# An attention and FFN block on one core: the softmax shift as the exponential's bias, FFN weights without low parts, and a checked fast path

## The chip, the cores and the metric

The kernel runs on one core of a Trainium2 chip. The metric is the device time in microseconds (us). TensorE is called PE, VectorE DVE, ScalarE ACT, GpSimd POOL, and SyncE, which issues most of the transfers, SP.

## The reference

Two sequences of 2048 rows of 256 pass through an attention block with 16 heads of 64 and then a gated FFN of hidden size 768. All data are float32; the FFN's weights are whole numbers from -127 to 127, divided by 127.

```
def attn(x):                       # x: layernorm of the input
    q, k, v = x @ Wq + bq, x @ Wk + bk, x @ Wv + bv       # 16 heads of 64
    a = softmax(q @ k.T / 8)                              # 2048 x 2048 for each head
    y = x + (a @ v) @ Wo + bo
    return (y - mean(y)) * rsqrt(var(y) + 1e-3) * gamma + beta

def ffn(x):                        # x: layernorm of the attention's result
    return (silu(x @ wg.T) * (x @ wu.T)) @ wd.T

x = x + layernorm(attn(layernorm(x)))
x = x + layernorm(ffn(layernorm(x)))
```

## The kernel before

**Precision.** Most matmul operands have the type float32r. For the projections, the scores and the FFN an operand is split into a high part (the value cast to float32r) and a low part (what the cast left), and a product takes three matmuls: high by high, high by low, low by high. ACT writes the high parts; DVE or POOL subtracts for the low ones.

**Attention.** The work is cut into 64 units `u = (b, p, c)`: sequence, pair of heads, block of 512 queries. `run_unit` writes the order of every engine's instructions by hand; only SP's order is left to a scheduler. The two heads of a pair use the two halves of PE's rows[...]. A unit has two halves (`j` = 0, 1) of eight key tiles of 128. A half runs as follows:

- `scores(u, kt)`: the scores of one key tile, keys by queries, into one of two PSUM buffers (`double`, tile `t`), and then the exponential by ACT (L671) into an SBUF tile `pt` (9 buffers). There are three pairs of matmuls for the split operands and a fourth pair (`unit` by `sh`), which adds each query's shift: minus its largest score.
- `max_pair(ahead, i)`: scores of the *next* unit, high parts only, queries by keys, into one of two other PSUM buffers (`xdouble`, tile `s`), and their maxima by DVE (L633) into `nm`. They stand in PE's order between the score tiles; the eighth of a half stands after the eighth score tile.
- `wo_half`: part of an earlier unit's output projection, added up by DVE (L264) with the inverse of the softmax's sum.
- `add_up(u, j)`: the sum over the eight `pt` tiles. POOL adds six to `accs` (L681, L684); DVE adds the other two into `two` (L688), and POOL adds `two` to `accs` (L691).
- in the first half, projections of later units' Q and K (`projs`) and of V (`v_tile`), and preparation of the FFN's weights (`prep_jobs`)
- `pv`: the product of `pt` and V for the eight tiles, into an `xdouble` buffer. After it, in the first half, `sum_up` and `first_half` bring out the sums of the unit behind, and SP gathers them into `few`; in the second half `cs_item` adds the two halves on DVE into `cf` (L230), and ACT and POOL split that into `cs`.

`shift_min` and `shift_row` make the shift: DVE takes the minimum over `nm`, at the start of the unit eight transposes on PE turn it into a row (L645), and ACT casts it to `sh` (L649). `inv_item`, in the second half, takes the reciprocals `rc` of the sums of the unit behind (L239).

**FFN.** Eight chunks of 512 rows, each with six steps of `gate_up` (six matmuls for gate and six for up), followed by `down` (four row tiles, 18 matmuls each). Between the steps stand pieces of other work: layer norms of the last four chunks (`own_job`), the end of the chunk before (`end_job`), and the last units of attention. The weights are brought on chip as high and low parts by `prep_jobs` during attention, go to memory, and are loaded again by `load_ffn`.

Of the kernel before, what the change touches and what calls it, by code (L numbers as in the profile page):

```python
# [16 lines left out]
P = 128  # L17
# [9 lines left out]

@with_exitstack
def kernel(
# [17 lines left out]
):  # L47
    nc = tc.nc
# [29 lines left out]
    wg_dram = dram.tile([P, 2, DC, HID], F32, name="wg_dram")  # L78
    wu_dram = dram.tile([P, 2, DC, HID], F32, name="wu_dram")
    wd_dram = dram.tile([P, 2, HC, D], F32, name="wd_dram")  # L80
# [4 lines left out]
    nbx = [const.tile([P, NT], F32, name=f"nbx{b}") for b in range(B)]  # L85

# [150 lines left out]
    def inv_item(u):  # L237
        t = op.tile([P, 2, QT], F32, tag="rc", name="rc")
        nc.vector.reciprocal(t, sums.pop(u))  # L239
        invs[u] = t  # L240
# [87 lines left out]
    def prep_jobs():  # L328
        jobs = []

        def piece(w, dst, o, i0):
# [9 lines left out]
            t = hd.tile([P, TT, D], F32, tag="ht", name="wt")[:, :2, :].bitcast(F32R)  # L341
            split(t, ps[:, : 2 * P])
            for k in range(2):
                nc.sync.dma_start(
                    out=dst[:, k, i0 : i0 + 2, o * P : (o + 1) * P],
                    in_=f32(t[:, k, :]).rearrange("p (i n) -> p i n", i=2),
                )

        for w, dst, no, ni in (
# [4 lines left out]
            for o in range(no):  # L354
                for i0 in range(0, ni, 2):
                    jobs.append(piece(w, dst, o, i0))
# [4 lines left out]
    def load_ffn(which):  # L361

        if which < 2:
            full = aw.tile([P, DC, S], F32R, tag=("xh", "xl")[which], name=f"fw{which}")
            full = full.rearrange("p c n -> p (c n)")
            n = 2 * DC * HID
            t = full[:, :n].rearrange("p (w c n) -> p w c n", w=2, c=DC)
            for w in range(2):
                for dc in range(DC):
                    nc.sync.dma_start(  # L370
                        out=f32(t[:, w, dc, :]), in_=(wg_dram, wu_dram)[which][:, w, dc, :]
                    )
                    yield None
# [3 lines left out]
        else:  # L377
            i = 2 * (which - 2)
            t = kp.tile([P, 2, 2, D], F32R, tag="T1", name=f"fw{which}")
            for w in range(2):  # L380
                nc.sync.dma_start(out=f32(t[:, w]), in_=wd_dram[:, w, i : i + 2, :])
                yield None
# [62 lines left out]
    with ExitStack() as actx:  # L445
# [4 lines left out]
        ptp = actx.enter_context(tc.tile_pool(name="ptp", bufs=9))  # L450
# [9 lines left out]

        unit_f = op.tile([P, 2, QB], F32, tag="rr", name="unit_f")[:, 0, :P]
        nc.gpsimd.memset(unit_f, 0.0)
        for e in range(2):
            nc.gpsimd.memset(unit_f[e * K : e * K + 1, :], 1.0)
        unit = bw.tile([P, P], F32R, name="unit")
        nc.scalar.copy(unit, unit_f)

        n8 = bw.tile([P, QT, P], F32, name="n8")
        nc.gpsimd.memset(n8, 0.0)

        wqk, wv, KT, QN, SH, V, nm, pts = ({} for _ in range(8))
# [147 lines left out]

# [15 lines left out]
        def shift_min(u):  # L635
            nc.vector.tensor_reduce(
                n8[:, :, 0 : K + 1 : K].rearrange("p q e -> p e q"), nm.pop(u), AX.X, ALU.min
            )

        def shift_row(u):  # L640

            ps = double()
            for qt in range(QT):
                for h in range(2):
                    nc.tensor.transpose(  # L645
                        ps[:, h, qt * K : (qt + 1) * K], n8[half(h), qt, :], ident[half(h), half(h)]
                    )
            SH[u] = bw.tile([P, QB], F32R, tag="sh", name="sh", bufs=2)
            nc.scalar.copy(  # L649
                SH[u].rearrange("p (q h r) -> p h q r", h=2, r=K),  # L650
                ps[:, :, : QT * K].rearrange("p h (q r) -> p h q r", r=K),
            )
# [525 lines left out]
```

## Time and profile before

| | |
|---|---|
| median of 3 runs | 2960.65 us (2960.57 to 2961.78) |
| the profiled execution's own time | 2961.08 us |
| its span, first to last instruction | 2959.3 us |
| attention | about 2725 us, the FFN the rest |
| busy: PE, DVE, ACT, POOL | 2876.9, 2102.9, 1467.1, 2444.7 us |
| exponentials (L671) | 1024, mean 1027 ns |
| maxima (L633) | 1024, mean 1225 ns |
| POOL's adds to `accs` (L684) | 636, mean 2548 ns |

Busy time is the time in which an engine had at least one instruction running. A group's mean is the time of one instruction.[...]

### The profile page before, as it was taken

How to read it: one execution, taken by the hardware profiler on the slowest of the kernel's cores; microseconds unless marked ns; L12 is line 12 of the kernel's file. 1: busy time of each engine (PE TensorE's matmuls, PEld its weight loads, DVE VectorE, ACT ScalarE, POOL GpSimd, SP SyncE). 2: the span in 40 equal slices, each digit the busy share in tenths (PEclk: the TensorE clock that was granted, in tenths of full speed). 3: DMA queues.
4: the chain of work that ended last, by engine and by line, in shares of the span. 5: the costliest groups of instructions: out<-in, count | busy, mean ns of one | idle time of the engine just before them, and what ended most of it. 6: DMA issues, size and time to landing. Idle time of an engine off the chain costs nothing.

```text
span 2959.3 us, 48771 instructions
## 1 busy us (share of the span) xinstructions
PE 2876.9 (97%) x19492; PEld 1742.6 (59%) x19492; DVE 2102.9 (71%) x2701; ACT 1467.1 (50%) x1740; POOL 2444.7 (83%) x1399
## 2 busy tenths in 40 slices
PE   7999999999999999989999999999999999999998
PEld 5555565556555565555655655555655555555787
DVE  6776677777777777766677767777677767774653
ACT  4545454544445444554455545555455445554443
POOL 4999878888788878877799989998799889888453
PEclk9999999999999999999999999999999999999999
DMA  2000000000000001010000001000000000012000
GB/s 59 19 12 11 14 12 12 12 15 5 17 10 14 9 12 31 5 35 10 26 21 10 7 10 33 5 20 24 5 6 24 21 1 31 23 58 72 29 29 29
DMA packets 125428, 59.14 MB, mean 20 GB/s; under 512 B 77232, under 2 KB 118448, under 8 KB 124816
## 3 DMA queue, kind: packets, MB, share of 16 engines
q1 hardware_dynamic: 124992, 55.62, 7.0%
q8 instruction: 152, 2.49, 0.4%
q0 software_dynamic: 208, 0.40, 0.1%
q14 instruction: 76, 0.62, 0.1%
HBM read 37.89 MB, written 17.83 MB: 19 GB/s over the span
## 4 chain that ended last, share of the span: by engine, by line
PE 85%; DVE 5%; POOL 4%; ACT 3%; issue 1%; DMA 1%; SPq 1%; ACTq 0%; DVEq 0%; POOLq 0%
PE t L670 32%; PE s L701 28%; PE s L626 8%; PE t L579 5%; PE t L604 3%; POOL accs L684 2%; ACT pt L671 2%; PE fp L1002 2%; PE s L199 2%; PE gp L975 2%; PE up L975 2%; PE t L253 2%; DVE two L688 1%; DVE nm L633 1%; DVE acc L264 1%
## 5 line engine op out<-in xcount | busy, mean ns | idle before, releaser
L684 POOL TENSOR_TENSOR accs<-accs,pt 128x1024 f32<-128x1024 f32 x636 | 1620.6, 2548 | 313.8 <-ACT pt L671 268.8
L633 DVE TENSOR_REDUCE nm<-s 128x2 f32<-128x1024 f32 x1024 | 1219.1, 1225 | 500.6 <-PE s L626 500.3
L671 ACT ACTIVATE pt<-t 128x1024 f32<-128x1024 f32 x1024 | 1049.8, 1027 | 184.7 <-PE t L670 117.8
L670 PE MATMUL t<-QN,KT 64*128 64x512 f32 x6144 | 916.0, 403 | 4.7 <-ACT pt L671 3.0
L701 PE MATMUL s<-pt,v 128*64 128x512 f32 x4096 | 908.1, 596 | 0.0
L670 PEld LDWEIGHTS t<-QN,KT 64*128 64x128 f32 x6144 | 521.2, 185 | 244.2 <-ACT pt L671 180.3
L701 PEld LDWEIGHTS s<-pt,v 128*64 128x64 f32 x4096 | 283.0, 137 | 538.4 <-issue 525.7
L626 PE MATMUL s<-KT,QN 64*128 64x512 f32 x2048 | 421.7, 408 | 5.6 <-DVE cf L230 4.1
L670 PE MATMUL t<-sh,unit 64*128 64x512 f32 x2048 | 405.8, 392 | 0.0
L691 POOL TENSOR_TENSOR accs<-accs,two 128x1024 f32<-128x1024 f32 x128 | 305.9, 2390 | 18.5 <-DVE two L690 7.5
L688 DVE TENSOR_TENSOR two<-pt 128x1024 f32<-128x1024 f32 x128 | 309.4, 2417 | 0.0
L223 ACT COPY rr<-s 128x1024 f32<-128x1024 f32 x63 | 63.9, 1015 | 430.2 <-PE s L199 417.0
L626 PEld LDWEIGHTS s<-KT,QN 64*128 64x128 f32 x2048 | 193.4, 185 | 108.4 <-issue 54.4
L649 ACT CAST sh<-t 128x512 fp32r<-128x512 f32 x64 | 37.6, 588 | 420.7 <-PE t L645 420.7
L670 PEld LDWEIGHTS t<-sh,unit 64*128 64x128 f32 x2048 | 192.9, 184 | 51.1 <-ACT sh L649 0.6
L264 DVE SCALAR_TENSOR_TENSOR acc<-t,rc,acc 128x256 f32<-128x256 f32 x500 | 206.9, 476 | 19.9 <-PE t L253 13.0
L579 PE MATMUL t<-xh,wqk 128*128 128x512 f32 x512 | 184.5, 421 | 18.2 <-ACT pt L671 10.5
L681 POOL TENSOR_TENSOR accs<-pt 128x1024 f32<-128x1024 f32 x64 | 154.9, 2420 | 0.5 <-ACT pt L671 0.5
L989 POOL TENSOR_TENSOR hT<-hf,hT 128x512 fp32r<-128x512 f32 x48 | 62.0, 1291 | 107.6 <-ACT hT L988 107.5
L579 PEld LDWEIGHTS t<-xh,wqk 128*128 128x128 f32 x512 | 99.6, 195 | 54.0 <-ACT pt L671 22.8
L589 ACT ACTIVATE QN<-t,bq_sb 128x512 fp32r<-128x512 f32 x64 | 44.1, 689 | 157.2 <-PE t L579 157.2
L253 PE MATMUL t<-wo,cs 64*128 64x256 f32 x1500 | 114.4, 285 | 2.0 <-ACT pt L671 1.8
(167 smaller groups left out, 2167.6 us busy)
## 6 DMA issues: line engine op xcount, KB each, us to landing
few<-rr SPq DMA_DIRECT2D x512, 0.5 KB, 2.0
xc<-in_L_attn_x_dram SPq DMA_DIRECT2D x8, 512.0 KB, 4.0
xT_dram<-hn SPq DMA_DIRECT2D x16, 256.0 KB, 2.1
out_dram<-o SPq DMA_DIRECT2D x14, 256.0 KB, 2.1
xT<-xT_dram SPq DMA_DIRECT2D x3, 1024.0 KB, 5.7
attn_dram<-acc SPq DMA_DIRECT2D x5, 512.0 KB, 2.6
acc<-in_L_attn_x_dram SPq DMA_DIRECT2D x4, 512.0 KB, 8.8
raw_w<-in_L_attn_Wq_dram SPq DMA_DIRECT2D x16, 128.0 KB, 2.2
```

What stands on the lines that cost most here:

```text
L253: nc.tensor.matmul(ps[e][:, i * D : (i + 1) * D], t[half(e), ci, s], w[half(e), wi, :], start=k == 0, stop=k == 2,)
L264: nc.vector.scalar_tensor_tensor(a, ps[e][:, i * D : (i + 1) * D], inv[:, e, q : q + 1], a, ALU.mult, ALU.add)
L579: nc.tensor.matmul(ps[:, k, :], w[:, wi, dc, :], xx[:, dc, s], start=n == 0, stop=n == 5)
L626: nc.tensor.matmul(s[:, e, :], QN[u][half(e), 0, qt * P : (qt + 1) * P], KT[b, p, kc][half(e), 0, :], start=True, stop=True,)
L633: nc.vector.tensor_reduce(nm[u][:, :, qt, kc : kc + 1], s, AX.X, ALU.max, negate=True)
L670: nc.tensor.matmul(ps[:, e, :], w, r, start=n == 0, stop=n == 3)
L671: nc.scalar.activation(pt, ps, AF.Exp, scale=QSCALE)
L681: nc.gpsimd.tensor_tensor(accs[u], todo[0], todo[1], ALU.add)
L684: nc.gpsimd.tensor_tensor(accs[u], accs[u], t, ALU.add)
L688: nc.vector.tensor_tensor(two, p8[n], p8[n + 1], ALU.add)
L691: nc.gpsimd.tensor_tensor(accs[u], accs[u], two, ALU.add)
L701: nc.tensor.matmul(pvs[u][half(e), 0, :], v[:, kt % 4, n : n + K], pt[:, e, :], start=kt % 8 == 0, stop=kt % 8 == 7,)
```

## The change

**Shift.** The score tiles lose the fourth pair of matmuls. The shift is now one number for the unit: minus its largest score over both heads, all its queries and all keys, times 1/8, plus 40. It enters the exponential as a bias, a column of 128 equal values. `shift_out` takes the minimum over `nm` on DVE into a column and sends it through memory: one transfer writes it to `m_dram`, the next reads it back as a row into all partitions (`mb`). `shift_in`, after the second half's `add_up` in the order of DVE and before `cf`, takes the minimum over the row (128 columns) and scales it with a `tensor_scalar`. The transposes, the `sh` cast, `unit` and `n8` are gone.

**Order in a unit.** The next unit's maxima stand between the first six score tiles of a half, the last two after the eighth. The `cs` split of the unit behind stands after the second score tile instead of before the first. `pt` has 10 buffers instead of 9. In the second half POOL adds five tiles and DVE three (two DVE additions instead of one).

**Checks.** `inv_item` gets a POOL instruction that adds `rc` into `inverse`. Each weight piece's low part is reduced to its largest absolute value in `wlow`, and is no longer stored. In the FFN's 17th step `verdict` compares the sum of the inverses with 2^80 and the low parts with zero, gathers the outcome of the 128 partitions through memory, and writes 1 or 0 to `good`.

**FFN.** Only the high parts of the weights are stored, loaded and used: `gate_up` has four matmuls for gate and four for up instead of six and six, `down` 12 for a row tile instead of 18.

**The end.** The former kernel is now `fast_path`. Behind it every engine loads `good` into a register and compares it; if it is 0, `general_path` (some 790 lines, a whole kernel for the same reference that shifts each query by its own maximum and uses split weights) computes the output anew.

```diff
     def inv_item(u):
         t = op.tile([P, 2, QT], F32, tag="rc", name="rc")
         nc.vector.reciprocal(t, sums.pop(u))
+        nc.gpsimd.tensor_tensor(inverse, inverse, t, ALU.add)
         invs[u] = t
...
-            t = hd.tile([P, TT, D], F32, tag="ht", name="wt")[:, :2, :].bitcast(F32R)
-            split(t, ps[:, : 2 * P])
-            for k in range(2):
-                nc.sync.dma_start(
-                    out=dst[:, k, i0 : i0 + 2, o * P : (o + 1) * P],
-                    in_=f32(t[:, k, :]).rearrange("p (i n) -> p i n", i=2),
-                )
+            t = hd.tile([P, TT, D], F32, tag="ht", name="wt")
+            hi = t[:, :1, :].bitcast(F32R)[:, 0, :]
+            nc.scalar.copy(hi, ps[:, : 2 * P])
+            nc.vector.tensor_tensor(t[:, 1, :], ps[:, : 2 * P], f32(hi), ALU.subtract)
+            nc.vector.tensor_reduce(
+                wlow[:, k : k + 1], t[:, 1, :], AX.X, ALU.max, apply_absolute_value=True
+            )
+            nc.sync.dma_start(
+                out=dst[:, i0 : i0 + 2, o * P : (o + 1) * P],
+                in_=f32(hi).rearrange("p (i n) -> p i n", i=2),
+            )
...
-        ptp = actx.enter_context(tc.tile_pool(name="ptp", bufs=9))
+        ptp = actx.enter_context(tc.tile_pool(name="ptp", bufs=10))
...
-        def shift_min(u):
...
-        def shift_row(u):
...
+        def shift_out(u):
+
+            n1 = bw.tile([P, 1], F32, tag="n1", name="n1", bufs=2)
+            nc.vector.tensor_reduce(
+                n1, nm.pop(u).rearrange("p e q c -> p (e q c)"), AX.X, ALU.min
+            )
+            d = m_dram[units.index(u) % 2]
+            nc.sync.dma_start(out=d.rearrange("(p o) -> p o", o=1), in_=n1)
+            t = shift[u] = bw.tile([P, P], F32, tag="mb", name="mb", bufs=2)
+            nc.sync.dma_start(out=t, in_=d.partition_broadcast(P))
+
+        def shift_in(u):
+
+            n1 = bw.tile([P, 1], F32, tag="n2", name="n2", bufs=2)
+            nc.vector.tensor_reduce(n1, shift[u], AX.X, ALU.min)
+            t = bw.tile([P, 1], F32, tag="sh", name="sh", bufs=2)
+            nc.vector.tensor_scalar(t, n1, QSCALE, HEADROOM, ALU.mult, ALU.add)
+            shift[u] = t
...
-            for n in range(4):
+            for n, (ki, qi) in enumerate(((0, 0), (0, 1), (1, 0))):
                 for e in range(2):
                     h = half(e)
-                    w, r = (
-                        (k[h, 0, s], q[h, 0, :]),
-                        (k[h, 0, s], q[h, 1, :]),
-                        (k[h, 1, s], q[h, 0, :]),
-                        (unit[h, :], sh[h, :]),
-                    )[n]
-                    nc.tensor.matmul(ps[:, e, :], w, r, start=n == 0, stop=n == 3)
-            nc.scalar.activation(pt, ps, AF.Exp, scale=QSCALE)
+                    nc.tensor.matmul(
+                        ps[:, e, :], k[h, ki, s], q[h, qi, :], start=n == 0, stop=n == 2
+                    )
+            nc.scalar.activation(pt, ps, AF.Exp, scale=QSCALE, bias=shift[u])
...
-            n = 4 if u == last else 6
+            n = 4 if u == last else 6 - j
...
-            shift_row(u)
-            if cs:
-                drain(cs.pop())
...
-                    if ahead and i < 7:
+                    if ahead and i < 6:
                         max_pair(ahead, 8 * j + i)
                     scores(u, 8 * j + i)
-                if ahead:
-                    max_pair(ahead, 8 * j + 7)
+                    if i == 1 and cs:
+                        drain(cs.pop())
+                for i in (6, 7) if ahead else ():
+                    max_pair(ahead, 8 * j + i)
                 if j == 1:
                     if ahead:
-                        shift_min(ahead)
+                        shift_out(ahead)
                     if behind:
                         inv_item(behind)
...
                 else:
+                    if ahead:
+                        shift_in(ahead)
                     cs.append(cs_item(u))
...
-                for wi, xi in ((0, 0), (0, 1), (1, 0)):
+                for xi in range(2):
...
-            for n, (hi, wi) in enumerate(((0, 0), (0, 1), (1, 0))):
+            for n in range(2):
...
+    def verdict():
+
+        t = op.tile([P, 4], F32, tag="few", name="ok")
+        nc.vector.tensor_reduce(
+            t[:, 0:1], inverse.rearrange("p e q -> p (e q)"), AX.X, ALU.max
+        )
+        nc.vector.tensor_scalar(t[:, 0:1], t[:, 0:1], MOST, None, ALU.is_le)
+        nc.vector.tensor_reduce(t[:, 1:2], wlow, AX.X, ALU.max)
+        nc.vector.tensor_scalar(t[:, 1:2], t[:, 1:2], 0.0, None, ALU.is_equal)
+        nc.vector.tensor_tensor(t[:, 2:3], t[:, 0:1], t[:, 1:2], ALU.mult)
+        nc.sync.dma_start(out=ok_dram.rearrange("(p o) -> p o", o=1), in_=t[:, 2:3])
+        row = op.tile([1, P], F32, tag="cf", name="row")
+        nc.sync.dma_start(out=row, in_=ok_dram.rearrange("(o n) -> o n", o=1))
+        yield
+        yield
+        yield
+        nc.vector.tensor_reduce(t[0:1, 3:4], row, AX.X, ALU.min)
+        nc.vector.tensor_copy(good, t[0:1, 3:4])
...
+def tile_attn_ffn_sandwich_kernel(tc: tile.TileContext, *args):
+    nc = tc.nc
+    with tc.tile_pool(name="good", bufs=1) as pool:
+        good = pool.tile([1, 1], I32, name="good")
+        fast_path(tc, *args, good)
+        value = nc.values_load(good[0:1, 0:1], min_val=0, max_val=1)
+        with tc.If(value < 1):
+            general_path(tc, *args)
```

## The prediction

> **What bounds the kernel now.** I read the page first, then the chain of waits, then the timelines of one unit. [...]Columns of the groups: total busy, mean ns, then idle time before.
>
> ```profile
> PE 2876.9 (97%) x19492; PEld 1742.6 (59%) x19492; DVE 2102.9 (71%) x2701; ACT 1467.1 (50%) x1740; POOL 2444.7 (83%) x1399
> PE 85%; DVE 5%; POOL 4%; ACT 3%; issue 1%; DMA 1%; SPq 1%; ACTq 0%; DVEq 0%; POOLq 0%
> L684 POOL TENSOR_TENSOR accs<-accs,pt 128x1024 f32<-128x1024 f32 x636 | 1620.6, 2548 | 313.8 <-ACT pt L671 268.8
> L671 ACT ACTIVATE pt<-t 128x1024 f32<-128x1024 f32 x1024 | 1049.8, 1027 | 184.7 <-PE t L670 117.8
> L670 PE MATMUL t<-sh,unit 64*128 64x512 f32 x2048 | 405.8, 392 | 0.0
> L589 ACT ACTIVATE QN<-t,bq_sb 128x512 fp32r<-128x512 f32 x64 | 44.1, 689 | 157.2 <-PE t L579 157.2
> ```
>
> PE looks full, and the 2048 shift matmuls look like 406 us. The chain in the last unit, where no maxima run between the score tiles, shows another limit:
>
> ```profile
> 2690.37 1.21 PE t L670 x7
> ...
> 2691.67 1.04 ACT pt L671
> ...
> 2692.75 1.22 PE t L670 x6
> ```
>
> Two score buffers give a loop: matmuls 1.21, exponential 1.03, hand-overs 0.13, together 2.37 us for two tiles, so 1.19 us a tile. Now DVE and POOL around the end of a unit (start, length, what ran, wait in brackets):
>
> ```profile
> 1519.55 1.23 DVE L633 TENSOR_REDUCE nm<-s 128x2 f32<-128x1024 f32 x1 [1.16 <-PE s L626]
> 1520.81 0.19 DVE L636 TENSOR_REDUCE n<-nm 128x8 f32<-128x32 f32 x1
> 1521.19 0.20 DVE L239 RECIPROCAL rc<-few 128x8 f32<-128x8 f32 x1 [0.18 <-issue]
> 1521.52 1.66 DVE L264 SCALAR_TENSOR_TENSOR acc<-t,rc,acc 128x256 f32<-128x256 f32 x4
> 1523.10 2.46 DVE L688 TENSOR_TENSOR two<-pt 128x1024 f32<-128x1024 f32 x1
> 1527.31 0.69 DVE L230 TENSOR_TENSOR cf<-s,rr 128x512 f32<-128x512 f32 x1 [1.75 <-PE s L701]
> 1527.99 2.39 DVE L633 TENSOR_REDUCE nm<-s 128x2 f32<-128x1024 f32 x2
> ```
>
> ```profile
> 1512.21 15.57 POOL L684 TENSOR_TENSOR accs<-accs,pt 128x1024 f32<-128x1024 f32 x6 [1.83 <-ACT pt L671]
> ```
>
> DVE has 1.75 us to spare before cf, and cf frees the PSUM buffer for the second maximum of the next unit. POOL adds all through this stretch. In the FFN:
>
> ```profile
> 2885.00:2935.00 50.00, 50.00 (x293) 44.16 (x291) 18.02 (x56) 20.69 (x38) 20.55 (x16) 1.00 0.07 22
> 2735.00:2885.00 150.00, 138.90 (x790) 120.74 (x789) 91.35 (x362) 66.58 (x126) 78.25 (x62) 0.97 0.09 29
> ```
>
> The busy columns are PE, PEld, DVE, ACT, POOL: PE alone is the limit in the last 50 us, and has DVE close behind before.
>
> [...]the two at 1523.10 takes 2.46 us where the one at 2724.57, with POOL idle, takes 1.22. The POOL add in front of it ended at 1524.48, two ended 1.08 later, and the POOL add then waiting ended at 1527.78, 2.22 after that. [...]L589, with such a bias, takes 689 ns, the plain cast of that size (L649) 588.
>
> **The change, part by part.**
>
> *Scores.* One of four matmul pairs goes (0.23 us a pair: eight matmuls in 0.93), the exponential gets a pointer bias (+0.09). The loop is 2.37-0.23+0.09 = 2.23, so 1.117 us a tile against 1.191 measured in this half (first to eighth start, 1511.04 to 1519.38): the gain is 0.07 a tile, not 0.4. The row transposes (0.39 a unit) and the sh cast go too.
>
> *Second half.* The first exponential starts 0.23 earlier, the eighth 0.23+7x0.074 = 0.7 earlier. The last two maxima are now both issued after the eighth tile, where one was: the first of them starts 0.7 earlier than the row at 1519.55, the second 1.16 later (pitch of the pair at 1527.99), so DVE finishes 0.46 later than now. PV needs the buffer of the first of them: 1518.85+1.23+0.1 = 1520.18, against 1520.25 in the chain. **PE gains nothing in this half.**
>
> *POOL's new wait.* In the built order the addition to `inverse` stands on POOL before the second half's adds, and it waits for rc on DVE. Queued behind it are five adds, two's add, the weight and cs subtractions and the next half's adds. The adds now start at 1512.21; they will start at 1521.39+0.46, plus 0.07 hand-over, 0.2 for the addition (8 columns, priced by POOL's 4-column additions) and 0.08: 1522.2. Does POOL bound the unit then? Its adds end 14 us on, at 1536.1, in time for the pt buffers (the seventh exponential of the next half, about 1537.4); the following half's adds end near 1556, and it idles until the next rc at about 1563. No.
>
> *DVE's longer tail.* The second half gives DVE another add. The first, ready at 1523.56, waits for POOL's add until 1524.6 and ends 1.08 later, 1525.68; [...]the second add ends at 1529.0, 3.3 us long. The new minimum over 128 columns (about 0.35 with gaps, from the 0.19 of 32 columns) and the one-column tensor_scalar (0.2) follow, then cf at 1529.55 to 1530.25: 2.25 us later than now, with PE as before. Behind cf stand the next maxima; behind the second maximum, in PE's order, the second score tile.
>
> *First half of the next unit.* PE now stalls. After cf, four maxima at 1.16 must pass before the sixth; then its score tile 0.23+0.96, then three exponentials at 1.12. With cf ending 3.3 us after PV's end, the eighth exponential ends at 3.3+4.7+1.3+3.4 = 12.7 or so, against 11.4 now: +1.4 us. A unit near 1977 backs this: a cf 2.28 late made its eighth exponential 1.84 late, with the transposes and fourth pair still in. 62 units: +87. Seven units with three V tiles wait for DVE to free their buffers, about +2 each: +14. The last unit has no maxima: -1.5. Together **+99**.
>
> *DMA.* shift_out adds two SP transfers a unit, one behind the other; the nearest rows land in 2.0 to 2.2 us (few, raw_w). From 1521.3 they are back by about 1526, under the two adds until 1529.0, so 0. If each took over 3.8 us they would show. In SP's order few, long issued, precedes them.
>
> *FFN.* 48 gate/up steps lose four matmuls of 0.23: 44 us. 32 down tiles lose six of 18 (2.14 us): 23. In the last stretch PE is alone and all of its share (21) counts; in the first 150 us PE falls to 93 of busy time beside DVE's 91, in order, so I count two thirds of 46. Sum **-50**, between -35 and -67.
>
> *Rest.* The pieces' extra reductions, the halved stores and loads, the tenth pt buffer and verdict's seven small DVE instructions lie beside longer work: 0; uncovered, the reductions cost 18x0.35 = 6. One fewer POOL add a unit (2.5) is spent inside POOL's new idle time: 0. The end adds a register load, a compare-and-branch and a jump over the general path. No row shows them[...]. Estimate +4, from +1[...] to +8[...]; a gain is excluded, since the end has only additions.
>
> Sum: 99-50+4 = +53 on the profiled execution's 2961.08 (span 2959.3 and 1.8 around it; the median 2960.65 is the same within 0.5), so **3013**.
>
> **Rivals.**
> [...]Then it waits for the next POOL add, some 1.8 us, and so does cf: 62x1.8 = +112 more, 3125. The page allows it; no small tensor_scalar in SBUF runs beside POOL in this trace, so one column is open.
> [...]With 1.23 us (the uncontended L690) it ends at 1527.0, cf is at 0.2 late, and the first half gains: -0.39-0.23-0.52, +0.09 for the last exponential, +0.5 for the cs cast now inside the tiles, about -0.55. 62x0.55 = 34, with FFN and end 2882. It decides where the unit loses less than 0.65 us, an add of about 2.6 us. For it: an L690 beside a shorter POOL operation took 2.13. Against: POOL's row of adds without a gap.
> *It runs the general path.* That would about double the time. The condition, worked out from the reference's inputs in float64, is far off: the largest accumulated inverse is about 2^10, the limit 2^80, and weights are whole numbers to 127, which I take as exact in the high part. 2 in 100.
>
> **How the numbers follow.** My case 45 in 100 (2975 to 3060 alone: 0.4 us a unit either way, the FFN's bounds, the end's); [...]the faster cases 27; the general path 2; within 0.2%, about what a measurement here can tell from no change, 4. Faster 0.27, same 0.04, slower 0.69. The range, 2890 to 3130, leaves out the tails of both outer cases.
>
> **What would show it.** Right: POOL's inverse addition idle before it on DVE's rc, some 9 us a unit; the second add (the group two<-two,pt) near 3.3 us; cf no longer waiting for PV; the second score tile of a unit waiting for cf; pt near 1.12 us; FFN steps at 1.84 us of PE. Wrong: two<-two,pt near 1.3 to 2, cf still waiting for PV, or DVE idle on a DMA before shift_in.

## The result, and the profile after

After: **3421.01 us** (median of 4 runs, 3415.91 to 3427.27); before, on the same chip: 2960.61 us (2958.86 to 2961.78). The ratio is 1.1557, interval 1.1531 to 1.1582: slower by 460 us, where +53 was forecast and 3130 was the end of the range.

The page of the kernel after (busy time of the engines, clock granted in 40 slices, then the chain that ended last):

```profile
PE 2811.5 (82%) x16548; PEld 1588.2 (47%) x16548; DVE 2280.3 (67%) x2917; ACT 1495.5 (44%) x1675; POOL 2347.5 (69%) x1397
PEclk9999999999999999988999999999999999999988
PE 34%; DMA 20%; ACT 17%; POOL 12%; DVE 11%; issue 5%; ACTq 0%; SPq 0%; POOLq 0%; DVEq 0%
```

PE has 2944 fewer matmuls and is busy for 65 us less, yet the span grew from 2959.3 to 3413.8. The chain, of which PE had 85% before, now lies on **DMA for 20%**. Before, that was 1%. The stages, from the last PV and the first and last gate matmul: attention ends at 3195.7 instead of 2723.8 (**+471.9**), the FFN to its last gate takes 193.7 instead of 214.3 (**-20.6**), what follows 23.5 instead of 20.3 (**+3.2**). The sum is 454.5, the difference of the spans. The forecast had +99, -50 and +4.

The waits (who waited for whom: total us, how many, the longest) name the place:

```profile
ACT pt L1472 <- DVE sh L1456: 882.7, 64, 15.0
POOL inverse L1056 <- DVE rc L1055: 832.7, 63, 28.4
PE s L1431 <- DVE cf L1046: 403.3, 62, 7.1
DVE n L1454 <- DMA mb<-m_dram: 297.5, 64, 12.5
```

The first is 13.8 us a unit. Of these some 9 aren't due to the trip: with the early shift below the same wait is still 569.7 us, 8.9 a unit, since ACT has nothing to exponentiate while PE does PV. The second is new, as forecast. The third is PE standing 6.5 us a unit for cf. The fourth says why: DVE stands some 4.6 us a unit for the shift to come back, and cf stands behind that on DVE. Of such a wait the forecast had none. The chain at the end of one unit (start, length, what):

```profile
1739.47 0.20 DVE n L1443
...
1739.68 8.11 DMA m_dram<-n
...
1747.81 4.08 DMA mb<-m_dram
...
1751.91 0.30 DVE n L1454
...
1752.23 0.15 DVE sh L1456
1752.38 0.61 DVE cf L1046
...
1753.04 0.79 PE s L1431 x2
```

No engine's work stands in this chain between the column of minima (1739.67) and the reduction of what came back (1751.91): 12.2 us of two transfers, one behind the other. Their issues (us to landing last):

```profile
few<-rr SPq DMA_DIRECT2D x512, 0.5 KB, 2.0
mb<-m_dram SPq DMA_DIRECT2D x64, 64.0 KB, 4.7
m_dram<-n SPq DMA_DIRECT2D x64, 0.5 KB, 7.7
```

`few`, which I took as the nearest row, moves as many bytes in a quarter of the time. The timeline of DVE and POOL in the same stretch (start, length, what ran, wait before it):

```profile
1740.12 0.20 POOL L1056 TENSOR_TENSOR inverse<-inverse,rc 128x8 f32<-128x8 f32 x1 [11.81 <-DVE rc L1055]
1740.28 13.81 POOL L1485 TENSOR_TENSOR accs<-accs,pt 128x1024 f32<-128x1024 f32 x5
1741.75 1.98 DVE L1489 TENSOR_TENSOR two<-pt 128x1024 f32<-128x1024 f32 x1
1743.84 3.21 DVE L1491 TENSOR_TENSOR two<-two,pt 128x1024 f32<-128x1024 f32 x1
1751.91 0.28 DVE L1454 TENSOR_REDUCE n<-mb 128x1 f32<-128x128 f32 x1 [4.86 <-DMA mb<-m_dram]
1752.23 0.15 DVE L1456 TENSOR_SCALAR sh<-n 128x1 f32<-128x1 f32 x1
1752.30 0.68 DVE L1046 TENSOR_TENSOR cf<-s,rr 128x512 f32<-128x512 f32 x1
```

The second add takes 3.21 us amid POOL's adds, where 3.3 was forecast (the 2.22 and 1.08 of the trace of before). The one-column tensor_scalar took 0.15 us while a POOL add ran, so it didn't wait for that add; in 61 of the 64 units a POOL add runs all through it, and its mean is 154 ns. Then DVE waits 4.86 us, cf follows, and with it the score tiles. An instruction that waits holds up those behind it on its engine here: PV is done at 1745.45, but cf, behind DVE's wait and sh, starts at 1752.30; ACT has written the half's tiles by 1738.03, but POOL's five adds, behind inverse, start at 1740.28. Averaged over the core, the reason hides: POOL's busy share fell to 69%, DVE's to 67%.

The stall costs more than its length. Two stretches by window (length, then busy us of PE, PEld, DVE, ACT, POOL, and the granted clock), the first right after such a stall, the second at the start of a unit's second half, where PE had no stall:

```profile
1705.00:1711.00 6.00, 5.46 (x26) 4.34 (x28) 5.19 (x5) 3.85 (x4) 5.92 (x4) 0.50 0.01 3
1728.00:1737.00 9.00, 8.48 (x64) 5.02 (x60) 6.95 (x6) 8.18 (x9) 0.31 (x1) 1.00 0.07 3
```

PE gets half its clock for about 6 us: the chain's first score tiles stand 1.71 us apart, later ones 1.12 (1.12 is the length of an exponential, so PE isn't the limit there). The granted clock is 0.50 in the 6 us from 1752 and from 1800 as well, each behind a stall of PE for cf (6.47 and 6.86 us).

### The profile page after: what moved, and what is told of

It is laid out like the page before. It is cut to its first block, busy times and chain, and to the rows that moved or that the text cites. A ratio compares the mean times of both kernels' runs of the same rounds, so it can differ in the third digit from the quotient of the medians.

```text
span 3413.8 us, 43168 instructions
## 1 busy us (share of the span) xinstructions
PE 2811.5 (82%) x16548; PEld 1588.2 (47%) x16548; DVE 2280.3 (67%) x2917; ACT 1495.5 (44%) x1675; POOL 2347.5 (69%) x1397
## 3 DMA queue, kind: packets, MB, share of 16 engines
HBM read 39.72 MB, written 15.50 MB: 16 GB/s over the span
## 4 chain that ended last, share of the span: by engine, by line
PE 34%; DMA 20%; ACT 17%; POOL 12%; DVE 11%; issue 5%; ACTq 0%; SPq 0%; POOLq 0%; DVEq 0%
ACT pt L1472 16%; DMA m_dram<-n 12%; PE s L1502 11%; PE t L1469 10%; POOL accs L1485 7%; DMA mb<-m_dram 7%; DVE nm L1438 5%; PE t L1385 4%; PE s L1431 4%; PE t L1410 2%; POOL accs L1492 1%; PE s L1015 1%; DVE cf L1046 1%; DVE two L1489 1%; POOL accs L1482 1%
## 5 line engine op out<-in xcount | busy, mean ns | idle before, releaser
L1438 DVE TENSOR_REDUCE nm<-s 128x2 f32<-128x1024 f32 x1024 | 1200.8, 1221 | 601.7 <-PE s L1431 600.4
L1472 ACT ACTIVATE pt<-t,sh 128x1024 f32<-128x1024 f32 x1024 | 1119.5, 1116 | 1040.3 <-DVE sh L1456 882.7
L1485 POOL TENSOR_TENSOR accs<-accs,pt 128x1024 f32<-128x1024 f32 x573 | 1517.6, 2648 | 40.8 <-ACT pt L1472 0.7
L1469 PE MATMUL t<-QN,KT 64*128 64x512 f32 x6144 | 1036.0, 446 | 54.8 <-ACT pt L1472 39.2
L1431 PE MATMUL s<-KT,QN 64*128 64x512 f32 x2048 | 456.2, 462 | 414.7 <-DVE cf L1046 403.3
L1469 PEld LDWEIGHTS t<-QN,KT 64*128 64x128 f32 x6144 | 603.5, 208 | 385.9 <-ACT pt L1472 290.3
L1056 POOL TENSOR_TENSOR inverse<-inverse,rc 128x8 f32<-128x8 f32 x64 | 13.1, 205 | 832.7 <-DVE rc L1055 832.7
L1431 PEld LDWEIGHTS s<-KT,QN 64*128 64x128 f32 x2048 | 217.7, 209 | 615.3 <-DVE cf L1046 430.4
L1489 DVE TENSOR_TENSOR two<-pt 128x1024 f32<-128x1024 f32 x128 | 275.4, 2152 | 0.0
L1454 DVE TENSOR_REDUCE n<-mb 128x1 f32<-128x128 f32 x64 | 18.3, 286 | 297.5 <-DMA mb<-m_dram 297.5
L1491 DVE TENSOR_TENSOR two<-two,pt 128x1024 f32<-128x1024 f32 x67 | 208.1, 3105 | 6.9
```

The source lines that it names most:

```text
L1431: nc.tensor.matmul(s[:, e, :], QN[u][half(e), 0, qt * P : (qt + 1) * P], KT[b, p, kc][half(e), 0, :], start=True, stop=True,)
L1438: nc.vector.tensor_reduce(nm[u][:, :, qt, kc : kc + 1], s, AX.X, ALU.max, negate=True)
L1469: nc.tensor.matmul(ps[:, e, :], k[h, ki, s], q[h, qi, :], start=n == 0, stop=n == 2)
L1472: nc.scalar.activation(pt, ps, AF.Exp, scale=QSCALE, bias=shift[u])
L1485: nc.gpsimd.tensor_tensor(accs[u], accs[u], t, ALU.add)
L1489: nc.vector.tensor_tensor(two, p8[n], p8[n + 1], ALU.add)
```

## The experiments

Medians over the 62 middle units, in us; T1 and T2 are the lengths from PV's end to PV's end of the first and second half, cf its start after PV's end of the unit before. PV's end is taken here about 0.36 us ahead of the end that the views give its last matmul, so that a cf of 0.40 follows PV without a wait:

| kernel | us | T1 | T2 | cf |
|---|---|---|---|---|
| before | 2960.6 | 22.23 | 18.53 | 0.40 |
| after | 3421.0 | 29.51 | 18.52 | 7.25 |
| early shift | 3061.4 | 23.46 | 18.52 | 1.74 |
| trip through SBUF | 3069.8 | 23.76 | 18.52 | 2.26 |
| PE kept busy | 3315.6 | 28.09 | 18.52 | 6.94 |
| early, inverse behind the adds | 2950.1 | 22.25 | 18.52 | 0.41 |
| early, one add | 3030.3 | 22.28 | 18.52 | 0.41 |
| early, both | 2944.7 | 22.20 | 18.51 | 0.41 |
| before, pointer bias | 2986.2 | 22.55 | 18.89 | 0.41 |
| shift by a matmul | 2954.4 | 22.01 | 19.09 | 0.41 |
| shift by a matmul, seven maxima | 2898.7 | 21.74 | 18.56 | 0.41 |
| after, inverse behind the adds | 3423.1 | 29.54 | 18.53 | 7.37 |

The whole loss of the kernel after is in T1.

**Is it the trip?** Theory: the transfers set cf's time. Rivals: POOL's wait, DVE's adds. Three runs: the trip started half a unit early, from the first half's maxima alone (the other half of the keys is left out of the maximum, also in the three versions built on it); the full column sent to a row in SBUF instead of to memory; and PE given matmuls to do while it waits for cf, all else as it was. The matmuls given to PE are pairs, one for each head, as in the score tiles: in the trace of before such a pair lasts 0.40 us (L670 at 2689.73) and one matmul of it 0.39, so the two run side by side.

```diff
 early shift
-                n1, nm.pop(u).rearrange("p e q c -> p (e q c)"), AX.X, ALU.min
+                n1,
+                nm[u].rearrange("p e q c -> p (e q) c")[:, :, :n],
+                AX.XY,
+                ALU.min,
 ...
+                if j == 0 and ahead:
+                    shift_out(ahead, 2)
                 if j == 1:
-                    if ahead:
-                        shift_out(ahead)
 trip through SBUF
-            nc.sync.dma_start(out=d.rearrange("(p o) -> p o", o=1), in_=n1)
-            nc.sync.dma_start(out=t, in_=d.partition_broadcast(P))
+            r = bw.tile([1, P], F32, tag="mr", name="mr", bufs=2)
+            nc.sync.dma_start(out=r.rearrange("o (q n) -> o q n", n=1), in_=n1)
+            nc.sync.dma_start(out=t, in_=r[0:1, :].unsqueeze(1).to_broadcast([1, P, P]))
 PE kept busy (ahead of the second score tile of a unit)
+                        ps = double()
+                        for _ in range(26):
+                            for e in range(2):
+                                nc.tensor.matmul(
+                                    ps[:, e, :],
+                                    KT[u[0], u[1], 0][half(e), 0, :P],
+                                    QN[u][half(e), 0, :],
+                                    start=True,
+                                    stop=True,
+                                )
```

> The changed kernel with the shift taken from the next unit's first eight maximum pairs alone (half of the keys), so that the two transfers leave at the end of the first half and have the whole second half to come back; shift_in stays where it is, and the number and kind of instructions too. Theory A (the trip through memory makes the forecast's miss): cf starts about 2.7 us after PV's end as forecast instead of 7.3, the granted clock is back near 0.99, and the time is about 3040: forecast 3013 with the FFN's gain at the 21 us and the end's cost at the 3 us that the changed kernel's trace shows. Theory B (the second DVE add and POOL's wait for rc make most of it): DVE's tail is as before without the trip, the time stays above 3300.

> The changed kernel with the column written to a row in SBUF instead of a row in memory, and broadcast from there; both transfers stay, the first still of 128 elements of 4 bytes. If the slow part is the write of single elements to memory (7.7 us), the first transfer falls to about the 2.0 us of the few transfers, which scatter single elements into SBUF, the row is back before the second DVE add ends, and the time is that of the kernel with the early trip, about 3040. If single elements are slow wherever they go, it stays near 3420.

> The changed kernel with 26 pairs of matmuls more at the start of each unit after the first, 0.23 us a pair, about 6 us, written into the second score tile's buffer ahead of its own matmuls and overwritten by them: PE is busy while it would wait for cf. Theory C (PE's clock halves after the idle time and the first four score tiles pay for it): the granted clock in the first 6 us after cf is 1.0 instead of 0.5, the eighth exponential of a unit ends about 1.5 us earlier, and the time falls by about 95 us to 3325. If the clock is no cause, the time stays within 10 us of 3420 or grows.

Measured: 3061.35 (ratio to before 1.0341, 1.0324 to 1.0358), 3069.80 (1.0364, 1.0347 to 1.0382), 3315.59 (1.1202, 1.1179 to 1.1226). Either way of getting the trip out of the path brings some 350 us, and the version through SBUF takes the maximum over all keys, as the kernel after does. Its two transfers, by the DMA issues:

```profile
mb<-mr SPq DMA_DIRECT2D x64, 64.0 KB, 3.9
mr<-n SPq DMA_DIRECT2D x64, 0.5 KB, 1.9
```

The same 128 single elements take 1.9 us to SBUF and 7.7 to memory. In the kernel after, 256 KB written to memory in longer runs (`xT_dram<-hn`) land in 2.1 us: in these transfers neither memory alone nor single elements alone are slow, the two together are.

Keeping PE busy through the same wait brought 105 us, though it adds matmuls. The mean clock rose from 0.921 to 0.989, and right after the wait it is whole:

```profile
1648.00:1654.00 6.00, 5.72 (x40) 3.25 (x40) 6.00 (x6) 5.17 (x7) 5.92 (x4) 1.00 0.00 0
```

Not all of the 105 is the clock. In this run the trip itself came back a little sooner (cf at 6.94 instead of 7.25, so up to 19 us over 62 units). That leaves some 86 of the 350 us as an estimate for the clock after the stall; the rest is the stall.

**What is left of it, POOL or DVE?** The early shift is still 100 us above before. Three versions of it: the addition to inverse issued behind POOL's adds of its half; one DVE add in both halves instead of two in the second, with POOL's wait kept; both.

```diff
 inverse behind the adds
         nc.vector.reciprocal(t, sums.pop(u))
-        nc.gpsimd.tensor_tensor(inverse, inverse, t, ALU.add)
         invs[u] = t
+    def inv_add(u):
+        nc.gpsimd.tensor_tensor(inverse, inverse, invs[u], ALU.add)
 ...
                 next(adding, None)
+                if j == 1 and behind:
+                    inv_add(behind)
 one add
-            n = 4 if u == last else 6 - j
+            n = 4 if u == last else 6
```

> The kernel with the early trip (shift from half of the keys), and the addition to inverse moved on POOL from ahead of the second half's adds to behind them. Theory D (POOL's wait for rc sets when its adds run, and so that DVE's second add finds POOL's next add in front of it): POOL's adds start about 9 us earlier, the second add falls from 3.2 us to 1.3 where POOL has run out of adds, cf starts about 2 us earlier, the eighth exponential of a first half ends about 0.8 us earlier, and POOL's backlog in the heavy units goes too: 3061 falls to about 3000. If the position of that addition is hidden, the time stays within 8 us of 3061.

> The kernel with the early trip, with one DVE add and six POOL adds in the second half as in the kernel before; POOL still waits for rc. If DVE's tail alone holds the unit (the forecast's step), cf starts at 0.4 us after PV's end again and the time falls by about 60 us to 3000. If POOL, started late, takes over (six adds from 13.8 us on end at 29.4, 10.9 us into the next unit, where the eighth exponential needs their buffer at about 9.8), the gain is eaten up: 3040 to 3070.

> The kernel with the early trip, one DVE add, and the addition to inverse behind POOL's adds. If DVE's tail and POOL's wait are all that is left of the loss in attention, the eighth exponential of a first half ends near 10.9 us instead of 11.4 in the kernel before, attention takes some 30 us less than there, and the FFN's 21 and the end's +3 bring about 2920 to 2940. If something else holds it, it stays above 2960.

Measured: 2950.06 (0.9967, 0.9954 to 0.9980), 3030.28 (1.0232, 1.0213 to 1.0251), 2944.72 (0.9944, 0.9925 to 0.9964): -111, -31 and -117. POOL's wait is nearly the whole of the rest, and **it makes the second add dear**. The group of that add (total busy us, mean ns, idle time before) with the early shift, then with inverse moved too, and the timeline of the latter:

```profile
L1494 DVE TENSOR_TENSOR two<-two,pt 128x1024 f32<-128x1024 f32 x67 | 211.5, 3157 | 6.9
```

```profile
L1496 DVE TENSOR_TENSOR two<-two,pt 128x1024 f32<-128x1024 f32 x67 | 94.8, 1415 | 6.9
```

```profile
2062.93 12.19 POOL L1490 TENSOR_TENSOR accs<-accs,pt 128x1024 f32<-128x1024 f32 x5 [4.91 <-ACT pt L1477]
2073.86 2.34 DVE L1494 TENSOR_TENSOR two<-pt 128x1024 f32<-128x1024 f32 x1
2076.31 1.23 DVE L1496 TENSOR_TENSOR two<-two,pt 128x1024 f32<-128x1024 f32 x1
2078.13 0.69 DVE L1046 TENSOR_TENSOR cf<-s,rr 128x512 f32<-128x512 f32 x1 [0.22 <-PE s L1507]
```

POOL now begins with the exponentials and is done at 2075.1, so the second add runs alone: 1.23 us, and cf waits for PV again. With inverse ahead, as in the timeline of the kernel after above, the same adds begin at the unit's end and lie across both of DVE's.

One add with POOL's wait kept gains much less, though the first half of its median unit is as short as before (22.28 against 22.23): it is the longer units that lose. The first of its waits on PE shows what remains:

```profile
PE t L1385 <- POOL wqk L1291: 48.0, 27, 5.2
```

That POOL is late with the low parts of the projections' weights, which stand in its queue behind the adds. This edit also hands POOL a sixth add in the same late stretch, so its 31 us aren't the price of DVE's second add alone. POOL's adds have 44% of that version's chain on the page; with inverse moved as well they have 11%.

**Do the two costs add?** The kernel after with inverse moved, the trip left as it is:

> The kernel after, with only the addition to inverse moved behind POOL's adds of its half; the trip through memory stays. Theory: where the trip is late by some 5 us a unit, POOL's wait is hidden behind it nearly whole, so that this gives about 3400 (3380 to 3425), though the same edit was worth 111 us once the trip was hidden. Rival: the two costs add up, since POOL's backlog acts in other stretches than the trip: 3421 less some 110, about 3310.

Measured: 3423.08 (1.1570, 1.1550 to 1.1589), no gain at all. The second add takes 1.23 us here too, and then DVE waits 7.64 us for `mb`:

```profile
1746.33 1.23 DVE L1493 TENSOR_TENSOR two<-two,pt 128x1024 f32<-128x1024 f32 x1
1755.19 0.29 DVE L1456 TENSOR_REDUCE n<-mb 128x1 f32<-128x128 f32 x1 [7.64 <-DMA mb<-m_dram]
```

The theory holds: the later of two arrivals sets cf. An edit worth 111 us once the trip is hidden is worth nothing before.

**The pointer bias.** The kernel before with a column of zeros as the exponential's bias:

```diff
+    zero = const.tile([P, 1], F32, name="zero")
-            nc.scalar.activation(pt, ps, AF.Exp, scale=QSCALE)
+            nc.scalar.activation(pt, ps, AF.Exp, scale=QSCALE, bias=zero)
```

> The kernel before with one edit: the exponential takes its bias from a column of zeros instead of none. Price of the pointer operand: the exponentials go from 1.027 to 1.12 us, and the two-buffer loop from 2.37 to 2.46 us for two tiles, +0.045 a tile, +46 us over 1024 tiles, 3006. If PE's order and not the loop sets the pace, it is hidden: within 5 us of 2960.

Measured: 2986.17 (1.0082, 1.0064 to 1.0101), +25, about half of the 46 that the theory gave. The exponential goes from 1027 to 1117 ns. A median unit is 0.6 us longer, the mean one 0.4 (42.21 against 41.78): the second half grows by the 0.36 of eight tiles at 0.045, the mean first half, which has the projections, by 0.09 only.

**A version that keeps the whole computation.** The column is put across the partitions by one fp32 matmul behind the fourth PV tile; inverse stands behind the adds; DVE has one add. The second version also puts the seventh maximum back between the score tiles; the third is the second without additions to inverse, low parts of weights, verdict, branch and general path.

```diff
+        def shift_across(u):
+            t = double()[:, 0, :P]
+            nc.tensor.matmul(t, shift[u].to_broadcast([P, P]), ident, start=True, stop=True)
+            shift[u] = t
 ...
                     pv(u, 8 * j + i)
+                    if i == 3 and j == 1 and ahead:
+                        shift_across(ahead)
 seven maxima
-                    if ahead and i < 6:
+                    if ahead and i < 7:
-                for i in (6, 7) if ahead else ():
+                for i in (7,) if ahead else ():
```

> The kernel after, with three edits: the unit's shift (from all its keys) goes to all partitions by one fp32 matmul of the column, broadcast as weights, against the identity, behind the fourth PV tile, so that no transfer is left in the shift's way; the addition to inverse stands behind POOL's adds of its half; DVE has one add of its own in both halves. Theory: the trip through memory and POOL's wait for rc are the whole of the loss in attention, so this gives what the version with the early shift of half of the keys and the same two edits gave, 2944.7, within 10 either way: the matmul costs PE about 0.25 us a unit (+16), the column's second input, now from PSUM, nothing, and there is no tail of transfers in queue SP. cf starts about 0.4 us after PV's end. Rival: the full maximum itself is what is dear, because its column comes only behind the last maximum and the matmul that waits for it stands in PE's order ahead of the last PV tiles: then PE waits there, PV ends 1 us a unit later, about 3005. A second rival: the value is back too late for DVE's cf all the same (DVE's tail is full), cf at 2 us after PV's end, about 3030.

> The version with the shift brought across by a matmul, and besides it the seventh maximum of a half back between the score tiles, as in the kernel before, so that one maximum is left behind the eighth tile, where the change put two. Theory: PV of the second half waits for the buffer of the first of the two, 11.8 us after the first half's PV ends where the exponentials would let it start at about 11.1; with one maximum left it starts there: -0.7 us a unit, -43, about 2900. Rival: DVE is then the later one (its eight maxima of 1.2 and the interleaved order set the pace of the score tiles): the exponentials of the half slip by what PV gains, and nothing changes (2945 within 10).

> The version with the shift across by a matmul and seven interleaved maxima, without anything that looks whether the fast path may be used: no additions to inverse, no low parts of the weights or their reductions, no verdict on DVE, no register load, no branch and no general path behind it. It prices the checks. Theory: the end costs 3 us and the verdict's stop of DVE in the FFN 5 to 10; the additions on POOL (0.2 us a unit) and the pieces' reductions lie beside longer work: 8 to 15 us less than the version with the checks. Rival: DVE's stop in the FFN is covered by PE's own work, so only the end is left: 3 us less.

Measured: 2954.44 (0.9980, 0.9972 to 0.9989), **2898.69 (0.9799, 0.9783 to 0.9815)**, 2891.21 (0.9764, 0.9747 to 0.9780). The timeline of the second:

```profile
2071.92 2.94 DVE L1494 TENSOR_TENSOR two<-pt 128x1024 f32<-128x1024 f32 x1
2072.73 0.49 PE L1453 MATMUL t<-ident,n 128*128 128x128 f32 x2
2074.79 0.28 DVE L1459 TENSOR_REDUCE n<-t 128x1 f32<-128x128 f32 x1
2075.10 0.15 DVE L1461 TENSOR_SCALAR sh<-n 128x1 f32<-128x1 f32 x1
2076.85 0.69 DVE L1046 TENSOR_TENSOR cf<-s,rr 128x512 f32<-128x512 f32 x1 [1.59 <-PE s L1507]
```

The matmul stands between PV tiles, takes 0.49 us, and DVE has the shift 1.6 us before cf can start. In the first version it lengthened the second half by 0.57 us (18.52 to 19.09), so it came out at the upper edge of what the theory gave. The seventh maximum's place is worth 56 us where 43 was expected: T2 loses 0.53, T1 0.27. This version is faster than both kernels, and leaves nothing out. Against before, its stages are -44.3 in attention, -22.1 in the FFN, +3.2 after it. The third version, which leaves out what looks at the sums and low parts, is 7.5 us faster, between the 3 of the rival and the 8 to 15 of the theory. The two profiled executions differ by 4.6: 1.6 in attention, nothing in the FFN, 3.0 at the end.

**The FFN.** First the kernel before with the high parts alone in the FFN, and nothing that looks at the low ones. Then the version of 2898.7 us and the kernel before, each with one Newton step instead of three in the FFN's layer norms (a step refines the inverse square root, so the norms' last digits are left out); and the version of 2898.7 us with the chain of a norm spread over two gate/up steps.

```diff
 high parts (in before)
-                for wi, xi in ((0, 0), (0, 1), (1, 0)):
+                for xi in range(2):
 ... (the same in down, halved stores and loads)
 short chain
-        for i in range(3):
+        steps = 3 if bank is None else 1
+        for i in range(steps):
 ...
-            d = rs if i == 2 else temp(5, "ny")
+            d = rs if i == steps - 1 else temp(5, "ny")
 split chain (the calls and buffers that go with it are left out here)
             y = d
+            if i == 0:
+                yield
 ...
-    OWN_AT = {2: OWN + 1, 14: OWN + 2, 24: OWN + 3}
+    OWN_AT = {2: OWN + 1, 12: OWN + 2, 22: OWN + 3}
```

> The kernel before with the FFN's part of the change alone: high parts of the weights stored, loaded and multiplied, no verdict, no check of the low parts, attention untouched. Forecast: -50, 2911. If the 21 us of the changed kernel are all that there is (DVE and the chains of the layer norms hold it), 2940. With verdict's transfers and the halved clock gone I take 2920.

> The version of 2898.7 us (shift across by a matmul, seven interleaved maxima), and in the FFN the reciprocal square roots of the layer norms with one Newton step in place of three, so that each of the 18 chains of small DVE instructions is six instructions of 0.2 us shorter; the norms' last digits are left out with them. Theory: the FFN got 21 of the 50 us because DVE, in order, holds hf behind these chains and PE waits for it; then 18 times 1.2 us less on DVE brings 10 to 20 us here. Rival: PE's idle time in the FFN comes from ACT and POOL between gate and down (silu, the cast, the low part), or from the clock: then 0 to 5 us.

> The kernel before with the same shorter chains in the FFN. Theory: there PE was the limit (9.5 of 10 us busy), so the same 22 us of DVE bring only 2 to 7 us; what DVE costs is a consequence of the fewer matmuls. Rival: DVE's chains were as much in the way before, and the edit brings the same 10 to 20 us in both; then they explain nothing of the missing gain.

> The version of 2898.7 us, with nothing left out: the chain of a layer norm on the attention's output is issued in two parts, in two gate/up steps, so that hf of the next step stands behind half a chain; the jobs of the third and fourth chunk begin two steps earlier to be done in time. Theory: hf is late by the part of the chain in front of it, and PE by what its two buffers don't cover; 11 of 18 chains are split, about 5 to 10 us less. Rival: DVE's total work sets the pace (no gain from another order): 2899 within 3.

Measured: 2936.30 (0.9914, 0.9898 to 0.9931), 2883.45 (0.9738, 0.9721 to 0.9754), 2951.87 (0.9966, 0.9952 to 0.9980), 2899.51 (0.9797, 0.9779 to 0.9815). The FFN's stage: 186.6, 178.1, 205.3, 192.3, where the kernel before has 214.3 and the version of 2898.7 us 192.2. The high parts alone thus bring 27.7 us in their stage, and 23 of the whole. Its first 125 us by window, in the kernel before, the version of 2898.7 us, and that one with the short chain:

```profile
2724.00:2849.00 125.00, 114.24 (x633) 97.20 (x634) 80.98 (x301) 57.25 (x107) 64.89 (x50) 0.97 0.16 55
```

```profile
2679.00:2804.00 125.00, 96.81 (x475) 77.87 (x472) 83.73 (x312) 60.51 (x113) 70.45 (x56) 0.88 0.17 55
```

```profile
2679.00:2804.00 125.00, 101.71 (x515) 80.41 (x512) 81.80 (x268) 64.34 (x120) 76.76 (x62) 0.93 0.17 55
```

PE's idle time went from 11 to 28 us, and its clock from 0.97 to 0.88: with less to do PE waits longer for the others, and its clock is lower as well. The short chain takes 14.1 us off the FFN, and 9.0 off that of before, more than the theory's 2 to 7: the rival is half right. The difference is 5 of the missing 29 us, and it isn't clear of chance: versions whose FFN is the same differ by up to 7.4 us in this stage (189.7 with the early shift and inverse behind the adds, 197.1 with the early shift and one add). Spreading a chain changed nothing (192.3 against 192.2), so the place of the chain inside a step isn't what holds PE. What is left is the amount of work that DVE, ACT and POOL have in a step; that is argued and not shown, and no run parts the three.

## Why the prediction was wrong, point by point

**DMA: 0.** This is the step that failed. It said "From 1521.3 they are back by about 1526". They took 12.4 us by landing times, not 4.7, so they came back about 4.9 us behind DVE's adds instead of under them. I took the price from `few`, of the same bytes, which lands in SBUF; a write of single elements to memory was on no row of the profile. It should have been an unknown with an upper bound, and my own condition ("If each took over 3.8 us they would show") its tipping point. Instead it carried no weight: neither range nor rivals hold a late transfer. Most of the signs that it gave for being right came true all the same (the second add at 3.1 us, the exponentials at 1.12, PE's score tile waiting for cf); of all its signs only "DVE idle on a DMA before shift_in" told the two apart. Its cost in attention is 346 us, the difference to the trip through SBUF (+471.9 against +126.1), or 362 to the early shift (+109.7), and some 86 of that, by the estimate above, is a term that I hadn't at all: the clock after PE's stall.

**Attention: +99.** With the trip out of the way it was +126 (through SBUF) or +110 (early). The first half's +1.4 (its terms, 12.7 less 11.4, give 1.3) was +1.5 or +1.2, the second half's nothing was nothing (18.53 to 18.52), cf's 2.7 us after PV's end was 2.3 or 1.7. The step that set it, a second add drawn out amid POOL's adds (3.3 us forecast, 3.1 measured), was right; that the sum comes so near is in part luck. Of the 110, the median unit has 76 (62 times 1.23), and the rest lies in longer units, for which I had 14.

**POOL's new wait: "Does POOL bound the unit then? ... No."** Wrong in part. POOL idles as forecast, though longer: 832.7 us before the addition to inverse, 13.2 a unit instead of some 9. But its adds no longer keep up with the exponentials: before, they waited 268.8 us for them, now 0.7. Their late start made DVE's second add long, and with one add the units with weights to split waited for POOL. I costed the add as DVE's longer tail; its length was about right, but what made it long was POOL's wait, and moving one addition cures it (111 us with the early shift).

**The rivals.** The first (22 in 100) had the one-column tensor_scalar wait for POOL's next add; with 154 ns beside POOL's adds it doesn't. The second add at 1.23 us, with cf in time, is the early shift with inverse behind the adds: -10 us against before in all, not -78. The FFN's missing gain is the smaller part of these 68 us: attention is 10.5 us longer than before there, where 34 less were forecast. The first half's eighth exponential does end 0.7 us earlier (10.71 against 11.41 after PV's end), but its PV starts when it did (15.52 against 15.50), so the 34 us counted for 62 units didn't come; with the seventh maximum back in its place PV starts at 15.01. The general path didn't run: no instruction of its lines is in the trace of the kernel after, so the low parts of these weights are zero.

**Pointer.** +0.09 an exponential is right (1116 against 1027). The loop fell to 1.12 us a tile as forecast.

**FFN: -50.** It was -20.6, -27.7 alone. Where nothing holds them the steps take PE 1.83 to 1.87 us, as forecast; to count two thirds of the first 150 us' gain was too much. PE's share of busy time there, 93 against DVE's 91, was the warning, and the clock falling with PE's idle time was not in the sum.

**End: +4.** This was my estimate, with no row of the profile behind it. Measured: +3.2, of which the version without branch and verdict shows 3.0. The verdict's two transfers, 7.03 and 4.42 us, stand in the chain, but DVE works on beneath them and waits 0.64 us for the row:

```profile
3286.88 0.27 DVE L1918 TENSOR_REDUCE ok<-row 1x1 f32<-1x128 f32 x1 [0.64 <-DMA row<-ok_dram]
```

The FFN's stage is 192.2 us with the verdict and without.

What stays open: how the FFN's missing gain, 22 to 29 us, divides between DVE's chains, ACT, POOL and the clock.

## What to carry to other kernels

A transfer's price is taken from a row of the same direction and the same pattern of elements (here 7.7 us into memory against 1.9 into SBUF), and where there is none, it is bounded from above and its tipping point goes into the range. When two things arrive for one instruction, removing the earlier one brings nothing: 0 us in one order, 111 in the other. An addition of 8 columns cost 111 us with the early shift by what stood behind it in its queue; it belongs behind the work that waits for nothing.

## What was not expected of the hardware

- 128 single elements, one a partition, land in 7.7 us in memory (7.0 for the verdict's), in 1.9 to 2.0 in SBUF; 256 KB in longer runs land in 2.1 us in memory. A 64 KB read back to all partitions takes 4.7 us from memory, 3.9 from a row of SBUF.
- In the kernel after, stalls of PE of some 6.5 us were followed by about 6 us at a granted clock of 0.50; matmuls with no use, put into the stall, made the kernel 105 us faster, some 86 of them by the clock (estimate: 105 less the up to 19 of the earlier cf).
- A one-column tensor_scalar in SBUF took 0.15 us beside a POOL add; DVE's second add of two SBUF inputs took 3.1 us amid POOL's row of adds, 1.23 alone.
